# A graph-attention layer on one core: sums and edge values moved behind the queries, folds by halves, 53 pick blocks in six groups

## The chip, the cores and the metric

The kernel runs on one core of a Trainium2 chip. The time is that of the device from start to end, in microseconds (us); before, the median of three runs is 1701.03 us (1699.82 to 1702.28). Engines: TensorE (PE, with its weight loads as PEld), VectorE (DVE), ScalarE (ACT), GpSimd (POOL) and SyncE (SP), which here only issues transfers.

## The reference, cut to what matters

There are 6250 nodes with 64 features and 206,250 edges, sorted by destination. Each edge scores its source's key against its destination's query, weighted by its own attributes, in four heads of 16; the source's value times that score is summed per destination, and a layer norm follows.

```python
Qh = (x @ Wq.T + bq).reshape(n, H, D)        # H = 4, D = 16
Kh = (x @ Wk.T + bk).reshape(n, H, D)
Vh = (x @ Wv.T + bv).reshape(n, H, D)
Ee = (edge_attr @ We.T + be).reshape(-1, H, D)
score = (Kh[src] * Qh[dst] * (1.0 / np.sqrt(D)) * Ee).sum(-1)
score = jnp.exp(jnp.clip(score, -5.0, 5.0))
msg = Vh[src] * score[..., None]
wV = jax.ops.segment_sum(msg, dst, num_segments=n)
x = _layernorm(x + wV.reshape(n, H * D))
```

## The kernel before

**Tiles, groups, steps.** Edges are cut into 1612 tiles of 128 edges; 8 tiles make a group, 202 groups in all (the last has 4 tiles). Two groups make a step up to group 193; the last eight groups are steps of their own. One loop runs over the groups g (0 to 202), written out by hand as one order of instructions for every engine; each engine works through its own instructions in that order and waits on semaphores for the others.

**Keys and values of the sources.** A table with key and value of every node (`kv_tab`) is written at the start. For most tiles POOL fetches the 128 rows of a tile by one indirect DMA (`gather_kv`, line 276), four steps ahead, into a ring of five buffers (`kvs`). The first 40 tiles are computed from gathered rows of x. For the last two tiles of some groups (`PICKED`) there is no gather: PE makes the rows itself, as a product of the node features, kept in SBUF as three bf16 parts (`parts`), with one-hot columns. Four tiles form a batch of 512 edges; the 6250 nodes are 25 blocks per batch, and each block takes three matmuls of 512 columns (two for the last block), 74 in all: `picks`, which are the line 725 rows `pick<-hot,parts`. The one-hots are made by VectorE (`hots`, line 681) from the batch's source numbers, which SP fetches spread over the partitions (`fetch_sources`, tile `srcs`) and which ScalarE and VectorE turn into three forms (`sources`, lines 241 to 243). When a batch's 25 blocks are done, VectorE keeps the right half (`picked`, line 703), four f32 products with the weights give key and value (`picked_kv`, rows `pick<-w,x`), and ScalarE writes them into the group's buffer (`place_kv`).

How many blocks a group does is set by `first_unit`: 35 blocks in four groups, 8.75 per group. `READY` has the group in which a batch's last block is done; its four tiles are the last two of the groups `READY + 4` and `READY + 5`. `LAST`, the number of batches, is 67, which is 268 tiles, and 1304 tiles are left to the gathers. The last pick runs in group 192.

**The work of one group.** PE computes the edge values for group g + 3 (`edges`, four 64 x 64 quadrants of the array, rows `room<-et,we_sb`), the queries for g + 2 by one-hot rows (`queries`, rows `qq<-to,qw`, two halves of 64 columns), and the transposed terms for g + 1 (`turn`, line 761). ScalarE copies the edge values out with their bias (`biased`, line 740). VectorE multiplies them with the queries (`terms`, line 755), multiplies with the keys and sums per head (`products`, lines 787 and 789); ScalarE makes the weights (`weigh`, lines 794 and 796), VectorE the messages (`message`, line 808), which are split into three bf16 parts (`keep` on ScalarE, `take` on VectorE).

**Sums and folds.** For a step that is done, PE sums the messages per destination with one-hot matrices (`sums`, rows `room<-msg,of`, the two groups in the two column halves of the array in turn). VectorE adds the result into a ring of eight 64-row slots (`add`, lines 873 to 881). Every eight groups or so (25 times in the run) four slots are brought to the layout of the output by f32 matmuls (`fold_blocks`: for each half u one product with `fold` and one with a shifted part of `ident`), and VectorE adds them to y (`add_blocks`, line 927). Edge values, sums and folded blocks lie in the two PSUM banks of one tile, `room`.

**Order in one group, as far as the change touches it.** VectorE: products, take, terms, one-hots for the next group, messages, more one-hots, then the adds. PE: the first four blocks of picks, turn, queries, the other blocks of picks, fold, sums, edges. SP: edge attributes (every second group), source numbers, query windows, key rows. Gathers are released by marks on PE's matmuls (`where`), two to six of them per group.

Of the kernel before, what the change touches and what calls it, by code (L numbers as in the profile page):

```python
# [24 lines left out]
NG = -(-T // G)  # L25
# [47 lines left out]
UNITS = NB // 2  # L73
# [3 lines left out]
LEAD = 1  # L77
# [2 lines left out]

def first_unit(g):

    return (g - LEAD) * 35 // 4


def when(k):

    return max(g for g in range(LEAD + 4 * k // 35 + 2) if first_unit(g) <= k)


LAST = max(m for m in range(1, NG) if when(UNITS * m - 1) + 8 < NG)
BEGIN = [when(UNITS * m) for m in range(LAST)]
READY = [when(UNITS * m + UNITS - 1) for m in range(LAST)]
PICKED = [(READY[m] + 4, READY[m] + 5) for m in range(LAST)]
ALL_PICKED = {g for pair in PICKED for g in pair}
assert len(ALL_PICKED) == 2 * LAST and min(ALL_PICKED) > XG
assert all(BEGIN[m + 1] > BEGIN[m] + 1 for m in range(LAST - 1))
# [37 lines left out]
def tile_gnn(ctx: ExitStack, tc: tile.TileContext, x, x_blocks, by_rows, xT, wT, bias, beT, weT, eT, src, src_rows, dst,  # L135
# [96 lines left out]
    def fetch_sources(m, pool):  # L232

        if m < LAST:
            SRC[m] = pool.tile([P, BATCH * P], I32, name="srcs")
            nc.sync.dma_start(SRC[m], src_rows[m:m + 1, :].to_broadcast([P, BATCH * P]))
# [67 lines left out]
    with tc.tile_pool(name="nodes", bufs=1) as nodes, \  # L304
# [13 lines left out]
        slots = [kv.rearrange("p t c -> p (t c)") for kv in kvs]  # L318
# [13 lines left out]
        for i in range(NB // CB):  # L332
            s = slice(i * CB * P, (i + 1) * CB * P)
# [25 lines left out]
        mark = []  # L359
# [267 lines left out]
    with tc.If(rv == 0) as branch:  # L627

        with tc.tile_pool(name="work", bufs=2) as work, \
# [92 lines left out]
            mark = []  # L722
# [28 lines left out]
            def terms(g):  # L751

                n = tiles_of(g) // 2
                TERM[g] = work.tile([P, G // 2, P], F32, name="term")
                nc.vector.tensor_mul(TERM[g][:, :n], EB.pop(g)[:, :n], qq[:, :n])  # L755
# [24 lines left out]
            def some_of(g):  # L780

                n = tiles_of(g)
                return [(0, n)] if g < NG - 1 else [(0, n // 2), (n // 2, n)]
# [8 lines left out]
            def weigh(g, lo, hi):  # L792
                score = SCORE.pop(g)
                nc.scalar.activation(score, score, AF.Relu, bias=five_p, scale=-1.0)  # L794
                WEIGHT[g] = weights[g % 3][:, lo:hi]
                nc.scalar.activation(WEIGHT[g], score, AF.Exp, bias=five_p, scale=-1.0)  # L796
# [105 lines left out]
            def slots(lo, apart):  # L902

                ks = [k for k in (lo, lo + 2) if k in touched]
                if not apart and len(ks) == 2 and ks[0] % RING < ks[1] % RING:
                    return [(0, 2, ring[:, ks[0] % RING:ks[1] % RING + 1:2, :])]
                return [((k - lo) // 2, (k - lo) // 2 + 1, ring[:, k % RING:k % RING + 1, :]) for k in ks]

            def fold_blocks(i):

                for u in range(2):
                    whole = slots(4 * i + u, False)
                    for lo, hi, what in whole:
                        product(folded[u * C:(u + 1) * C, lo:hi], fold, what, start=True, stop=False,
                                skip_group_check=True)
                    for lo, hi, what in slots(4 * i + u - 1, i == len(ENDS) - 1):
                        product(folded[u * C:u * C + SHIFT, lo:hi], ident[:, C:C + SHIFT], what,
                                start=hi > max(h for _, h, _ in whole), stop=True, skip_group_check=True)

            def add_blocks(i):  # L920

# [61 lines left out]
            for g in range(NG + 1):  # L983
                now, before = g < NG, g > 0
                todo, ahead = pieces(g), pieces(g + 1)
                going, where = [], []
                if g < 2:
                    going = alone(lots(4)[2 * g:2 * g + 2])
                elif now and step_of[g] + KVB - 1 < NS:
                    going = lots(step_of[g] + KVB - 1)  # L990
                    going = alone(going[:2] if g == groups_of(step_of[g])[0] else going[2:])
                if g % LG == 0 and g + 3 * LG < NG:
                    fetch_edges(g // LG + 3)
                if g + 1 in BEGIN[1:]:
                    fetch_sources(BEGIN.index(g + 1) + 1, work)
                if g + 4 < NG:
                    fetch_queries(g + 4)
                if g % 2 == 0 and g + 6 < NG:
                    fetch_keys(g + 6, work)
                done = [s for s in range(NS) if groups_of(s)[-1] + 2 == g]  # L1000
                parted = now and step_of[g] < WHOLE
                former = before and step_of[g - 1] < WHOLE
                fetch_blocks(g)
                where.append(mark[-1])
                if former:
                    keep(g - 1, 1)
                if now:
                    products(g, *some_of(g)[0])
                if former:
                    take(g - 1, 1)  # L1010
                if g + 1 < NG:
                    terms(g + 1)
                if now:
                    weigh(g, *some_of(g)[0])
                if g + 2 < NG:
                    biased(g + 2)
                for mc in ahead[:1]:
                    hots(*mc)
                if now:
                    message(g, *some_of(g)[0])  # L1020
                for lo, hi in some_of(g)[1:] if now else []:
                    products(g, lo, hi)
                    weigh(g, lo, hi)
                    message(g, lo, hi)
                if g + 4 < NG:
                    onehot_rows(g + 4, work.tile([3 * W, G, P], BF16, name="to", bufs=4))
                if parted:
                    keep(g, 0)
                for mc in ahead[1:]:
                    hots(*mc)  # L1030
                for s in done:
                    add(s)
                if g - 1 in FOLDS:
                    add_blocks(FOLDS[g - 1])
                if g - 1 in READY:
                    picked(READY.index(g - 1))
                if g - 2 in READY:
                    picked_kv(READY.index(g - 2))
                    place_kv(READY.index(g - 2))
                where.append(mark[-1])  # L1040
                two = by_two(todo)
                for some in two[:2]:
                    picks(some)
                    where.append(mark[-1])
                if g + 1 < NG:
                    turn(g + 1)
                if g + 2 < NG:
                    queries(g + 2)
                for some in two[2:]:
                    picks(some)  # L1050
                    where.append(mark[-1])
                if g in FOLDS:
                    fold_blocks(FOLDS[g])
                if g - 1 in ends and now:
                    sums(ends[g - 1])
                if g + 3 < NG:
                    edges(g + 3)
                where.append(mark[-1])
                if g + 4 < NG:
                    onehot_rows_rest(g + 4)  # L1060
                if g in BEGIN:
                    sources(BEGIN.index(g) + 1, *from_odd())
                for i, lot in enumerate(going):
                    gather((lot, where[i * len(where) // len(going)]))
                for h in ([g] if g < NG - 3 else []) + ([g + 1] if NG - 4 <= g < NG - 1 else []):
                    if h not in ends:
                        continue
                    s = ends[h]
                    t0 = STEPS[s][0] * G
                    for t in range(t0, t0 + tiles_in(s)):  # L1070
                        if t and t % KEYS == 0:
                            keys(t)
                    onehot_edges(s)
                    if s >= WHOLE:
                        widen(s)
                if g - 1 in READY:
                    biased_kv(READY.index(g - 1))
                if parted:
                    take(g, 0)
                if done:  # L1080

                    while closed < B - 2 and summed[closed] <= g:
                        spreads(closed)
                        closed += 1
                    if closed in BATCHES and closed > scaled:
                        roots(scaled, closed)
                        scales(scaled, closed)
                        scaled = closed
                    for _ in range(3):
                        if normed < scaled:  # L1090
                            norm(normed)
                            normed += 1
# [180 lines left out]
```

## Time and profile before

| | before |
|---|---|
| median of three runs | 1701.03 us |
| the profiled execution | 1701.22 us |
| its span, first to last instruction | 1699.4 us |
| mean granted TensorE clock | 0.982 |
| busy: PE, VectorE, ScalarE, POOL | 1641.8, 1525.8, 1097.8, 1272.5 us |
| gathers (line 276) | 1304, mean 946 ns |
| pick matmuls | 4958 |

A line of the timeline has start, length, engine, line, operation, what is written and read with shapes, the number of merged instructions, and in brackets how long the engine was idle before and what ended that. A line of the waits has who waited for whom, the total in us, how many times, and the longest. A line of the groups has busy time and mean length, then the idle time before. Matmul ends are modelled, so starts are to be compared.

### The profile page before, as it was taken

Reading aid. Unit: us, or ns where it says so; the run is one execution under the profiler, and the core shown is the slowest. Engines: PE = TensorE matmul, PEld = TensorE weight load, DVE = VectorE, ACT = ScalarE, POOL = GpSimd, SP = SyncE. Lnnn points to the kernel's source line nnn. Section 1 sums busy time; section 2 is a strip of 40 time slices with the busy share of each in tenths; the row PEclk is TensorE's granted clock in tenths of the full one; section 3 lists DMA queues with packets and bytes.
Section 4 is the critical chain, followed back from the end, with each engine's and each line's share of the span. In section 5 each row is a group of like instructions: output and inputs, shape, how many; then the busy total and the mean of one; then the engine's idle time right before and its main releaser. Section 6 shows DMA issues by size and latency. Waiting matters only on the chain.

```text
span 1699.4 us, 29987 instructions
## 1 busy us (share of the span) xinstructions
PE 1641.8 (97%) x10327; PEld 818.4 (48%) x10327; DVE 1525.8 (90%) x2588; ACT 1097.8 (65%) x1860; POOL 1272.5 (75%) x1354
## 2 busy tenths in 40 slices
PE   7799999999999999999999999999999999999975
PEld 6444444444444444444444444444444444444443
DVE  5699989899989899998998998989999999889986
ACT  3676666666666666666666666666666666666664
POOL 7777777777777777777777777777777777777775
PEclk9799999999999999999999999999999999999995
DMA  6744344343443434434434344443444433434341
GB/s 195 244 123 143 99 123 123 104 124 109 114 123 104 123 108 114 124 117 123 114 108 130 99 122 122 106 124 105 117 123 117 123 111 111 123 105 130 111 116 46
DMA packets 115090, 203.90 MB, mean 120 GB/s; under 512 B 55216, under 2 KB 55961, under 8 KB 114815
## 3 DMA queue, kind: packets, MB, share of 16 engines
q1 hardware_dynamic: 71484, 113.99, 22.1%
q0 software_dynamic: 43008, 86.86, 19.3%
q8 instruction: 83, 1.36, 0.3%
q10 hardware_dynamic: 436, 1.04, 0.3%
q14 instruction: 79, 0.65, 0.1%
HBM read 194.18 MB, written 7.59 MB: 119 GB/s over the span
## 4 chain that ended last, share of the span: by engine, by line
PE 80%; DVE 7%; DMA 7%; issue 2%; ACT 2%; POOL 1%; SPq 0%; DVEq 0%; ACTq 0%; POOLq 0%
PE pick L725 59%; PE room L725 11%; PE qe L761 5%; DMA kv<-kv_tab,src_i 4%; PE qq L725 3%; DMA srcs<-in_src_rows 2%; POOL kv L276 1%; DVE prod L787 1%; DVE msg L827 1%; DVE term L755 1%; PE ps L490 1%; DVE hot L681 1%; DVE score L789 1%; DVE qe L827 1%; DVE of L775 1%
## 5 line engine op out<-in xcount | busy, mean ns | idle before, releaser
L276 POOL DMA_INDIRECT kv<-kv_tab,src_i x1304 | 1233.1, 946 | 398.1 <-issue 173.8
L725 PE MATMUL pick<-hot,parts 128*128 128x512 bf16 x4958 | 1136.4, 380 | 0.0
L725 PEld LDWEIGHTS <-parts 128*128 128x128 bf16 x4958 | 459.5, 98 | 588.1 <-issue 90.3
L681 DVE TENSOR_TENSOR hot<-from,still 128x2560 bf16<-128x2560 bf16 (+4 forms) x415 | 481.7, 1164 | 2.4 <-ACT still L796 2.4
L822 ACT ACTIVATE msg<-qe 128x512 bf16<-128x512 f32 x400 | 237.8, 594 | 170.2 <-DVE qe L808 98.8
L740 ACT ACTIVATE eb<-room,be_col 128x512 f32<-128x512 f32 x202 | 136.8, 677 | 147.1 <-PE room L725 146.6
L262 ACT ACTIVATE to<-to,one_p 126x1024 bf16<-126x1024 bf16 x198 | 226.9, 1146 | 0.0
L256 ACT ACTIVATE to<-kb,minus_row 126x1024 bf16<-126x1024 uint8 x198 | 224.7, 1135 | 0.0
L794 ACT ACTIVATE score<-score,five_p 128x32 f32<-128x32 f32 x203 | 65.1, 321 | 147.8 <-DVE score L789 145.9
L761 PE MATMUL qe<-ident,term 128*128 128x128 f32 x806 | 125.7, 279 | 28.1 <-DVE term L755 26.4
L787 DVE TENSOR_TENSOR prod<-kv,qe 128x512 f32<-128x512 f32 x203 | 137.1, 676 | 12.0 <-PE qe L761 3.7
L789 DVE TENSOR_REDUCE score<-prod 128x32 f32<-128x512 f32 x203 | 138.5, 682 | 7.0
L827 DVE TENSOR_TENSOR qe<-qe,msg 128x512 f32<-128x512 f32 x200 | 138.2, 691 | 3.9 <-ACT msg L822 3.8
L808 DVE SCALAR_TENSOR_TENSOR qe<-still,kv 128x512 f32<-128x512 f32 x200 | 138.7, 693 | 0.8 <-ACT still L796 0.8
L827 DVE TENSOR_TENSOR msg<-qe,msg 128x512 bf16<-128x512 f32 x200 | 136.6, 683 | 3.1 <-ACT msg L822 2.6
L755 DVE TENSOR_TENSOR term<-eb,qq 128x512 f32<-128x512 f32 x202 | 136.6, 676 | 3.0 <-DMA kv<-kv_tab,src_i 2.6
L725 PE MATMUL room<-et,we_sb 64*64 64x256 f32 (+1 forms) x1616 | 136.2, 408 | 0.3 <-ACT eb L740 0.2
L761 PEld LDWEIGHTS qe<-ident,term 128*128 128x128 f32 x806 | 99.9, 143 | 75.8 <-DVE term L755 41.9
L243 DVE TENSOR_SCALAR odd<-srcs 128x512 int32<-128x512 int32 x66 | 30.2, 458 | 79.4 <-DMA srcs<-in_src_rows 79.3
L725 PE MATMUL room<-msg,of 128*64 128x192 bf16 (+1 forms) x1592 | 88.6, 251 | 1.6 <-DVE y L927 1.3
L725 PEld LDWEIGHTS <-of 128*64 128x64 bf16 (+1 forms) x1600 | 67.4, 110 | 39.0 <-issue 36.6
L241 ACT ACTIVATE from<-srcs,from_row 128x512 bf16<-128x512 int32 x66 | 47.3, 717 | 60.0 <-DMA srcs<-in_src_rows 60.0
(156 smaller groups left out, 1102.9 us busy)
## 6 DMA issues: line engine op xcount, KB each, us to landing
et<-in_eT SPq DMA_DIRECT2D x100, 512.0 KB
kb<-key_tab SPq DMA_DIRECT2D x101, 252.0 KB
kv<-kv_tab,src_i POOLq DMA_INDIRECT x1304
srcs<-in_src_rows SPq DMA_DIRECT2D x67, 256.0 KB
qw<-q_tab SPq DMA_DIRECT2D x202, 15.8 KB
kv_tab<-kv_sb SPq DMA_DIRECT2D x4, 640.0 KB
q_tab<-q SPq DMA_DIRECT2D x5, 480.0 KB
out<-y SPq DMA_DIRECT2D x2, 512.0 KB
```

Of the source, the lines that this page charges most:

```text
L256: nc.scalar.activation(TO[g][:, :n, :], KB.pop(g)[:, :n * P].rearrange("p (j e) -> p j e", j=n), AF.Square, bias=minus_row3[:3 * W])
L262: nc.scalar.activation(TO[g][:, :n, :], TO[g][:, :n, :], AF.Relu, bias=one_p[:3 * W], scale=-1.0)
L276: return nc.gpsimd.indirect_dma_start(out=kv_of(g)[:, j, :], out_offset=None, in_=kv_tab[:, :], in_offset=bass.IndirectOffsetOnAxis(ap=src ...
L681: nc.vector.tensor_tensor(HOT[k][:, lo_ - lo:hi_ - lo].rearrange("p b (a c) -> p b a c", c=2), pairs(from_)[:, None].to_broadcast(shape), ...
L725: mark.append(nc.tensor.matmul(*aps, **kw))
L755: nc.vector.tensor_mul(TERM[g][:, :n], EB.pop(g)[:, :n], qq[:, :n])
L761: nc.tensor.transpose(qe[g % 2][:, k:k + half + 1:half, :], TERM[g][:, k, :], ident)
L787: nc.vector.tensor_mul(prod, kv_of(g)[:, lo:hi, :C], qe[g % 2][:, lo:hi, :])
L789: nc.vector.tensor_reduce(SCORE[g], prod.rearrange("p g (h d) -> p g h d", h=H), axis=AX.X, op=OP.add)
L808: nc.vector.scalar_tensor_tensor(to.rearrange("p g (h d) -> p g h d", h=H), WEIGHT.pop(g)[:, :, :, None].to_broadcast([P, n, H, D]), LEAST ...
L822: nc.scalar.activation(part, left, AF.Copy)
L827: nc.vector.tensor_sub(left if i == 0 else part_of(g, 2)[1], left, part)
```

## The change

- `first_unit`: 53 blocks in six groups (8.833 per group) in place of 35 in four. The bound on the last batch is looser (`+ 5` for `+ 8`), and the last batch's tiles may be nearer to its last block (`min(4, NG - 2 - r - 1)`), so that its groups are 199 and 200. There are 69 batches; the last pick runs in group 196.
- `fold_blocks`: both halves' products with `fold` first, then both shifted ones.
- `fetch_sources`: issued two groups ahead of its use, not one.
- VectorE: the adds (`add`, `add_blocks`) stand right after the terms, ahead of one-hots and messages, and in the written order ahead of ScalarE's copy of the edge values.
- In group 200 the products stand behind the terms of group 201, not ahead of them.
- PE: fold, sums and edges come right behind the queries, ahead of the group's remaining picks.

```diff
 def first_unit(g):
-    return (g - LEAD) * 35 // 4
+    return (g - LEAD) * 53 // 6
 def when(k):
-    return max(g for g in range(LEAD + 4 * k // 35 + 2) if first_unit(g) <= k)
+    return max(g for g in range(LEAD + 6 * k // 53 + 2) if first_unit(g) <= k)
-LAST = max(m for m in range(1, NG) if when(UNITS * m - 1) + 8 < NG)
+LAST = max(m for m in range(1, NG) if when(UNITS * m - 1) + 5 < NG)
-PICKED = [(READY[m] + 4, READY[m] + 5) for m in range(LAST)]
+PICKED = [(r + k, r + k + 1) for r in READY for k in [min(4, NG - 2 - r - 1)]]
...
             def fold_blocks(i):
+                whole = [slots(4 * i + u, False) for u in range(2)]
                 for u in range(2):
-                    whole = slots(4 * i + u, False)
-                    for lo, hi, what in whole:
+                    for lo, hi, what in whole[u]:
                         product(folded[u * C:(u + 1) * C, lo:hi], fold, what, start=True, stop=False,
                                 skip_group_check=True)
+                for u in range(2):
                     for lo, hi, what in slots(4 * i + u - 1, i == len(ENDS) - 1):
                         product(folded[u * C:u * C + SHIFT, lo:hi], ident[:, C:C + SHIFT], what,
...
-                if g + 1 in BEGIN[1:]:
-                    fetch_sources(BEGIN.index(g + 1) + 1, work)
+                if g + 2 in BEGIN[1:]:
+                    fetch_sources(BEGIN.index(g + 2) + 1, work)
...
-                if now:
+                if now and g != NG - 2:
                     products(g, *some_of(g)[0])
                 if former:
                     take(g - 1, 1)
                 if g + 1 < NG:
                     terms(g + 1)
+                if g == NG - 2:
+                    products(g, *some_of(g)[0])
                 if now:
                     weigh(g, *some_of(g)[0])
+                for s in done:
+                    add(s)
+                if g - 1 in FOLDS:
+                    add_blocks(FOLDS[g - 1])
                 if g + 2 < NG:
                     biased(g + 2)
...
                 for mc in ahead[1:]:
                     hots(*mc)
-                for s in done:
-                    add(s)
-                if g - 1 in FOLDS:
-                    add_blocks(FOLDS[g - 1])
...
                 if g + 2 < NG:
                     queries(g + 2)
-                for some in two[2:]:
-                    picks(some)
-                    where.append(mark[-1])
                 if g in FOLDS:
                     fold_blocks(FOLDS[g])
                 if g - 1 in ends and now:
                     sums(ends[g - 1])
                 if g + 3 < NG:
                     edges(g + 3)
+                for some in two[2:]:
+                    picks(some)
+                    where.append(mark[-1])
                 where.append(mark[-1])
```

More of the change, by code (lines that the diff above doesn't have):

```diff
@@ L909, in fold_blocks @@
             def fold_blocks(i):
+                whole = [slots(4 * i + u, False) for u in range(2)]
                 for u in range(2):
-                    whole = slots(4 * i + u, False)
-                    for lo, hi, what in whole:
+                    for lo, hi, what in whole[u]:
                         product(folded[u * C:(u + 1) * C, lo:hi], fold, what, start=True, stop=False,
                                 skip_group_check=True)
+                for u in range(2):
                     for lo, hi, what in slots(4 * i + u - 1, i == len(ENDS) - 1):
                         product(folded[u * C:u * C + SHIFT, lo:hi], ident[:, C:C + SHIFT], what,
-                                start=hi > max(h for _, h, _ in whole), stop=True, skip_group_check=True)
+                                start=hi > max(h for _, h, _ in whole[u]), stop=True,
+                                skip_group_check=True)
             def add_blocks(i):
```

## The prediction

> **What bounds the kernel now.** I read the page first, then the waits, the queue of gathers in order of time, and the end of the run engine by engine. The page alone points at PE:
>
> ```profile
> span 1699.4 us, 29987 instructions
> PE 1641.8 (97%) x10327; PEld 818.4 (48%) x10327; DVE 1525.8 (90%) x2588; ACT 1097.8 (65%) x1860; POOL 1272.5 (75%) x1354
> L276 POOL DMA_INDIRECT kv<-kv_tab,src_i x1304 | 1233.1, 946 | 398.1 <-issue 173.8 <-PE pick L725 83.2 <-DMA kv<-kv_tab,src_i 66.7
> ```
>
> POOL's 75% misleads. 398.1 us of idle time over 1304 gathers is 0.305 us each, and the waits of POOL have nothing longer than that; rows of its timeline 28 gathers apart give the step:
>
> ```profile
> POOL kv L276 <- PE pick L725: 83.2, 273, 0.3
> ...
> 1650.14 0.94 POOL L276 DMA_INDIRECT kv<-kv_tab,src_i  x1 [0.30 <-issue]
> ...
> 1685.08 0.95 POOL L276 DMA_INDIRECT kv<-kv_tab,src_i  x1 [0.30 <-issue]
> ```
>
> (1685.08 - 1650.14) / 28 = 1.248 us per gather, 0.94 of it busy and 0.30 between two. So POOL issues gathers without a break, 1304 x 1.248 = 1627 us of them, up to 1686.0. Nothing in the run holds it back, and only fewer gathers shorten it. Whether that stream ends the run is seen in VectorE's timeline of the tail:
>
> ```profile
> 1636.64 0.69 DVE L787 TENSOR_TENSOR prod<-kv,qe 128x512 f32<-128x512 f32 x1
> ...
> 1683.09 0.69 DVE L787 TENSOR_TENSOR prod<-kv,qe 128x512 f32<-128x512 f32 x1 [3.13 <-issue]
> ...
> 1685.34 0.69 DVE L808 SCALAR_TENSOR_TENSOR kv<-still,kv 128x512 f32<-128x512 f32 x1
> ...
> 1693.88 0.32 DVE L955 TENSOR_SCALAR y<-y,stats,rstd 128x64 f32<-128x64 f32 x1
> ```
>
> The product at 1683.09 is that of group 200. The last gather for it is the fifth from the end (1685.08 - 4 x 1.248 = 1680.1, done at 1681.0, landed some 2 us later): VectorE sat 3.13 us for it. From there to the end of the span are 16.3 us. So before ends on the gathers, but with 3.1 us of slack only: PE, whose picks stop in group 192, is close behind. Both have to be priced.
>
> PE's tail, the turns of iterations 192 and 196, and the last sums but one:
>
> ```profile
> 1636.00 0.60 PE L761 MATMUL qe<-ident,term 128*128 128x128 f32 x4
> ...
> 1656.63 1.11 PE L761 MATMUL qe<-ident,term 128*128 128x128 f32 x4 [3.17 <-DVE term L755]
> ...
> 1687.24 3.57 PE L725 MATMUL pick<-kv,kv 128*128 128x64 f32 x16
> ```
>
> PE's timeline in the middle of the run, iterations back to back:
>
> ```profile
> 835.13 1.16 PE L725 MATMUL pick<-w,x 128*128 128x128 f32 x8
> 836.13 2.75 PE L725 MATMUL pick<-hot,parts 128*128 128x512 bf16 x12
> ...
> 842.93 0.43 PE L725 MATMUL room<-ring,fold 128*64 128x128 f32 x2
> 843.29 0.41 PE L725 MATMUL room<-ring,ident 128*31 128x64 f32 x4
> 843.63 0.43 PE L725 MATMUL room<-ring,fold 128*64 128x128 f32 x2
> 844.00 0.41 PE L725 MATMUL room<-ring,ident 128*31 128x128 f32 x2
> 844.33 0.85 PE L725 MATMUL room<-msg,of 128*64 128x192 bf16 x16
> 845.11 0.66 PE L725 MATMUL room<-et,we_sb 64*64 64x256 f32 x8
> 845.71 2.55 PE L725 MATMUL pick<-hot,parts 128*128 128x512 bf16 x11
> 848.09 0.60 PE L761 MATMUL qe<-ident,term 128*128 128x128 f32 x4
> 848.62 0.41 PE L725 MATMUL qq<-to,qw 126*64 126x512 bf16 x2
> 848.96 3.41 PE L725 MATMUL pick<-hot,parts 128*128 128x512 bf16 x15
> 852.30 0.66 PE L725 MATMUL room<-et,we_sb 64*64 64x256 f32 x8
> 852.89 2.76 PE L725 MATMUL pick<-hot,parts 128*128 128x512 bf16 x12
> ```
>
> Starts are what counts, as the ends are modelled. 11 picks followed by the turn take 848.09 - 845.71 = 2.38, so 0.2164 each. 15 picks followed by the edges take 852.30 - 848.96 = 3.34 against 15 x 0.2164 = 3.25: leaving the picks for narrow tiles costs 0.094. The two query matmuls (512 columns, one column half each) take 0.34 before the picks, where one stream of 512 columns is 0.216: going back to the picks costs 0.124.
>
> **The change, part by part.**
>
> *53 blocks in six groups.* 8.833 blocks per group in place of 8.75; with the looser bound on the last batch 69 batches of 25 blocks in place of 67. A batch is 24 x 3 + 2 = 74 picks and spares 4 gathers. POOL: 1304 - 8 = 1296 gathers, 8 x 1.248 = 10.0 us less. PE: 148 picks x 0.2164 = 32.0 us, two more blocks of eight f32 matmuls (836.13 - 835.13 = 1.0) 2.0 us. The picks now end in group 196, so four more iterations stand ahead of that point: each turn, queries and edges, 0.53 + 0.34 + 0.59 = 1.46, is 5.8, three sums at 0.78 and one fold at 1.40 are 3.7. Together the turn of iteration 196 would come at 1636.0 + 43.5 = 1679.5, were nothing saved.
>
> *Sums and edge values behind the queries.* In an iteration the picks were left for the sums or edges (0.094) and entered from the queries (0.124); now both go, and the step from queries to sums or to edges is new. The trace has no such step. Bounds: 0 (sums use the same column halves as the queries) and 0.124 (the dearest switch seen). To the edges I take 0.094, as from the picks, to the sums 0; sums come in every second iteration. Saved: 0.124 or 0.218, mean 0.171, in 195 iterations 33.3 us; ends 18.3 and 42.5. The Trainium skill ("TensorEngine Tiling (Array Packing)", Key Properties) says that a change of tiling mode drains the array and a change of tile does not; the 0.094 on leaving the picks agrees with it, and by it the sums' step is free and the edges' is not: 33.3 us again, with the low end out.
>
> *Folds by halves in turn.* A fold is 844.33 - 842.93 = 1.40 us: 0.36, 0.34, 0.37, 0.33. Halves do run side by side here: 16 sums of 192 columns take 0.78, one after the other they would be 16 x 192/512 x 0.2164 = 1.30. At best half of 1.40 goes, at worst nothing; each f32 product shows as two records, of which I expect one to overlap, so 0.35 in 24 folds, 8.4 us (0 to 16.8). The Trainium skill ("TensorE: Matmul & The Clock Gate", Part 3, The mechanism) has matmuls start and end strictly in program order; if the two records of a half stay next to each other, that too gives about half; no run here shows it yet.
>
> PE's sum: 1679.5 - 33.3 - 8.4 = 1637.8 for the turn of iteration 196 (ends 1620 and 1661). From that turn before took 1699.4 - 1656.63 = 42.8 us, of which 3.13 were the gather: 39.7. PE alone would end at 1677.5.
>
> *POOL's sum.* Product of group 200 at 1683.09 - 10.0 = 1673.1, and 16.3 after it: 1689.4. It is later than PE's 1677.5, so it decides, as long as PE's savings are over 30 us of the 41.7 I expect. What is late next is then the gathers again, and PE waits for them from about group 190 on.
>
> *Terms of the last group ahead of products (g = 200).* Its turn and the sums before then no longer stand behind the gather; the sums at 1687.24 could start with the messages at 1685.34 + 0.69 = 1686.03. 0 to 1.2 us; I take 1.0. Span 1688.4.
>
> *Source rows a group further ahead; adds right after the weights.* Rows of the waits, the fourth of the window 1560 to 1700 alone, the last of SP's queue:
>
> ```profile
> DVE odd L243 <- DMA srcs<-in_src_rows: 79.3, 35, 3.7
> ACT from L241 <- DMA srcs<-in_src_rows: 60.0, 37, 2.9
> PE qe L761 <- DVE term L755: 26.4, 19, 5.4
> ...
> PE qe L761 <- DVE term L755: 20.6, 8, 5.4
> ...
> SPq L216 <- PE room L725: 1177.7, 87, 18.7
> ```
>
> SP issues in bursts: the edge load waits for a PE edge block, and source rows, queries and keys go behind it. A fetch one group earlier leaves with the burst before where it was late, and with the same burst, early enough, where it was not. So VectorE's 79.3 us go; they were paid by slack mostly, PE waited 26.4 us in all for VectorE, 20 of it in the tail. I count nothing. The added work of VectorE and ScalarE is hidden by that:
>
> ```profile
> 800.00:1000.00 200.00, 199.28 (x1278) 96.45 (x1277) 182.57 (x294) 129.85 (x216) 151.23 (x161) 1.00 0.41 118
> ```
>
> (Columns: window, PE, PE's weight loads, VectorE, ScalarE, POOL.) And the timeline of one iteration:
>
> ```profile
> 846.28 0.38 SPq L236 DMA_DIRECT2D srcs<-in_src_rows  x1
> ...
> 850.34 0.43 DVE L243 TENSOR_SCALAR odd<-srcs 128x512 int32<-128x512 int32 x1 [2.71 <-DMA srcs<-in_src_rows]
> ...
> 855.04 0.68 DVE L755 TENSOR_TENSOR term<-eb,qq 128x512 f32<-128x512 f32 x1
> 855.14 0.67 ACT L740 ACTIVATE eb<-room,be_col 128x512 f32<-128x512 f32 x1
> ...
> 855.63 1.48 DVE L681 TENSOR_TENSOR hot<-from,still 128x2560 bf16<-128x2560 bf16 x1
> ...
> 855.77 0.66 PE L761 MATMUL qe<-ident,term 128*128 128x128 f32 x4
> ```
>
> 50 more blocks of one-hots at 1.48 / 5 = 0.30 are 15 us of VectorE in 1640, against 79 freed; without that cover VectorE, busy 182.57 of 200, would still be under POOL's pace. Two more fetches on SP (256 KB each) and ACT's two batches are idle time. The adds move ahead of one-hots and messages, which come under 1 us later, with the next picks over 4 us away.
>
> **The whole.** Span 1688.4 against 1699.4; outside the span lie 1701.22 - 1699.4 = 1.8 us, so 1690.2, and the profiled run was 0.2 over the median of 1701.03: 1690.0 us, 0.65% faster. About 0.2% (3.4 us) is what a measurement can tell from no change.
>
> **Rivals.**
>
> 1. *PE decides.* If the new step from queries costs the dearest switch everywhere and the folds win nothing, 18.3 us are saved, the turn is at 1661.2 and the end at 1661.2 + 39.7 - 1.0 = 1699.9, a time of 1701.7: no change. From 18 to 30 us saved the time falls from there to 1690. For it: PE's 97%. Against it: both switches are there in the rows above.
>
> 2. *A new wait in PE's queue; slower.* Sums and edges write the two banks that ScalarE's copy of the edge values (line 740) reads, and 15 picks now queue behind them. In the rows above that copy ends at 855.81 and the turn came at 855.77, sums or edges would want the banks 0.53 + 0.34 = 0.87 us after that: it suffices by 0.8. But the add, which reads the same banks, is now put ahead of the copy; if the copy waits for it, it comes about 0.4 later, after folds 1 us. Slower than before from 1677.5 - 1.0 + w over 1699.4 + 3.4, w = 26 us, 0.13 per iteration. At 0.35 in every second iteration, 34 us, the time is 1712. Against it: PE waited for VectorE's term only 19 times in 202, so it mostly runs behind, with the copy long done.
>
> 3. *The fetch is not earlier* (the burst still holds it), so VectorE keeps its 79.3 us: 182.57 + 9.3 of 200 us busy or waiting is 0.96 of the pace, still under POOL's. Time 1690 as well; it changes nothing here.
>
> **How the numbers follow.** POOL decides: 0.70 (rival 3 within it), 1688.5 to 1692. PE decides: 0.15, spread over 1691 to 1702. New wait: 0.12, 1702 to 1715. Anything else, 0.03. The range 1687 to 1700 leaves out rival 2 and the end of rival 1. Faster by 0.2%: 0.70 and over half of 0.15, 0.78; within 0.2%: 0.08; slower: 0.14.
>
> **What would show it.** Gathers x1296, still without a wait over 0.3, their last near 1676; picks x5106; the queries followed by sums within about 0.22 and by edges within about 0.31; a fold under 1.1; the waits for srcs nearly gone; a product of groups 195 to 200 that waits for a gather. Wrong: PE's row of waits with an entry for eb (line 740) or the add over 20 us, POOL rows with gaps over 0.3 in the middle, or picks that run to 1665 and no wait for gathers after them.

## The result, and the profile after

The changed kernel takes 1691.5 us, the median of six runs (1690.68 to 1692.92), against 1701.23 us (1699.82 to 1702.69, six runs) before: a ratio of 0.9943, 95% interval 0.993 to 0.9956. The profiled execution took 1691.6 us.

The page of the kernel after, its head and its costliest rows:

```profile
span 1689.7 us, 30289 instructions
PE 1623.6 (96%) x10491; PEld 842.8 (50%) x10491; DVE 1533.3 (91%) x2593; ACT 1106.1 (65%) x1870; POOL 1265.5 (75%) x1346
L276 POOL DMA_INDIRECT kv<-kv_tab,src_i x1296 | 1226.1, 946 | 395.2 <-issue 196.8
L725 PE MATMUL pick<-hot,parts 128*128 128x512 bf16 x5106 | 1148.8, 380 | 0.0
```

There are 1296 gathers and 5106 picks. 395.2 us of idle time over 1296 gathers is 0.305 us each, the same short gap as before: POOL still issues without a break. Its last gather, in its timeline after, and its longest row of waits for PE (total, times, longest):

```profile
1675.06 0.94 POOL L276 DMA_INDIRECT kv<-kv_tab,src_i  x1 [0.30 <-PE pick L725]
...
POOL kv L276 <- PE pick L725: 82.6, 271, 0.3
```

It ends at 1676.0, against 1686.0 before: the 10.0 us that eight gathers are worth. The stream starts at the same time in both (its first gather at 55.1 before and at 55.0 after). VectorE's timeline of the tail after, the products of the groups 196 to 200:

```profile
1642.93 0.69 DVE L787 TENSOR_TENSOR prod<-kv,qe 128x512 f32<-128x512 f32 x1 [1.54 <-PE pick L725]
...
1650.79 0.69 DVE L787 TENSOR_TENSOR prod<-kv,qe 128x512 f32<-128x512 f32 x1 [2.00 <-DMA kv<-kv_tab,src_i]
...
1659.94 0.68 DVE L787 TENSOR_TENSOR prod<-kv,qe 128x512 f32<-128x512 f32 x1
...
1666.96 0.68 DVE L787 TENSOR_TENSOR prod<-kv,qe 128x512 f32<-128x512 f32 x1
...
1674.07 0.68 DVE L787 TENSOR_TENSOR prod<-kv,qe 128x512 f32<-128x512 f32 x1
```

The product of group 200 starts at 1674.07, and 15.6 us later the span ends. The last product that waited for its gather is not this one but that of group 197, at 1650.79. From there the products come 9.15, 7.02 and 7.11 us apart. In a later run, in which the gathers do not decide (after with fewer gathers and the folds of before), the same products start at 1629.76, 1639.13, 1646.15 and 1653.27, so 9.37, 7.02 and 7.12 us apart: the last three groups run at their own pace, started by a gather. The gather for group 200, the fifth from the end, started at 1670.07. Before, the product followed the start of that gather by 3.0 us (1683.09 - 1680.09), so here the gather would have let it start at 1673.1, 1.0 us before it did. How long the products waited in all is in VectorE's waits after, first of the window 110 to 780, then of 780 to 1690:

```profile
DVE prod L787 <- PE qe L761: 22.2, 28, 1.8
```

```profile
DVE prod L787 <- PE pick L725: 32.9, 22, 4.6
DVE prod L787 <- DMA kv<-kv_tab,src_i: 30.2, 14, 5.0
DVE prod L787 <- PE qe L761: 3.9, 4, 1.5
```

Up to 780 us products waited for PE alone; behind it they waited for the gathers. The row that names the picks belongs with them, as a later run shows. The pace says the same. Two windows with the products (L787) alone, of the kernel before and then of the kernel after, give their number in brackets:

```profile
200.00:700.00 500.00, 42.09 (x62) 1.00 0.40 114
900.00:1600.00 700.00, 58.89 (x87) 1.00 0.41 116
```

```profile
200.00:700.00 500.00, 43.60 (x64) 1.00 0.42 118
900.00:1600.00 700.00, 57.86 (x85) 1.00 0.41 115
```

After, a group takes 500 / 64 = 7.8 us early and 700 / 85 = 8.2 later; before it took 500 / 62 = 8.06 and 700 / 87 = 8.05. A group after needs 8 - 4 x 8.833 / 25 = 6.587 gathers on average, and 6.587 x 1.248 = 8.22 us, which is the later pace. So PE now runs ahead at its own pace, uses up the stock of gathered rows, and is then held to the pace of the gathers. The stream of gathers decides the end, as before, but PE would now be done long before it, where it was close behind it.

### The profile page after: what moved, and what is told of

Same layout as the page of the kernel before. It is cut to its first block, busy times and chain, and to the rows that moved or that the text cites. A ratio compares the mean times of both kernels' runs of the same rounds, so it can differ in the third digit from the quotient of the medians.

```text
span 1689.7 us, 30289 instructions
## 1 busy us (share of the span) xinstructions
PE 1623.6 (96%) x10491; PEld 842.8 (50%) x10491; DVE 1533.3 (91%) x2593; ACT 1106.1 (65%) x1870; POOL 1265.5 (75%) x1346
## 4 chain that ended last, share of the span: by engine, by line
PE 80%; DVE 10%; issue 4%; DMA 3%; ACT 2%; POOL 0%; DVEq 0%; SPq 0%; ACTq 0%; POOLq 0%
PE pick L725 60%; PE room L725 10%; PE qe L761 5%; PE qq L725 3%; DMA kv<-kv_tab,src_i 2%; DVE hot L681 2%; DVE prod L787 1%; DVE msg L827 1%; DVE term L755 1%; PE ps L490 1%; DVE qe L808 1%; DVE score L789 1%; DVE qe L827 1%; DMA ones_tab<-ones 0%; DMA et<-in_eT 0%
## 5 line engine op out<-in xcount | busy, mean ns | idle before, releaser
L276 POOL DMA_INDIRECT kv<-kv_tab,src_i x1296 | 1226.1, 946 | 395.2 <-issue 196.8
L725 PE MATMUL pick<-hot,parts 128*128 128x512 bf16 x5106 | 1148.8, 380 | 0.0
L725 PEld LDWEIGHTS <-parts 128*128 128x128 bf16 x5106 | 484.0, 98 | 618.0 <-issue 77.9
L681 DVE TENSOR_TENSOR hot<-from,still 128x2560 bf16<-128x2560 bf16 (+4 forms) x414 | 492.9, 1195 | 2.5 <-ACT still L796 2.4
L787 DVE TENSOR_TENSOR prod<-kv,qe 128x512 f32<-128x512 f32 x203 | 137.4, 677 | 96.1 <-PE pick L725 32.9
L725 PE MATMUL qq<-to,qw 126*64 126x512 bf16 x396 | 80.9, 405 | 0.0
L725 PEld LDWEIGHTS <-of 128*64 128x64 bf16 (+1 forms) x1600 | 73.8, 110 | 14.1 <-issue 5.0
L725 PEld LDWEIGHTS pick<-w,x 128*128 128x128 f32 x552 | 72.1, 192 | 15.6 <-ACT pick L714 6.7
```

The lines of the kernel that those rows point to most:

```text
L276: return nc.gpsimd.indirect_dma_start(out=kv_of(g)[:, j, :], out_offset=None, in_=kv_tab[:, :], in_offset=bass.IndirectOffsetOnAxis(ap=src ...
L681: nc.vector.tensor_tensor(HOT[k][:, lo_ - lo:hi_ - lo].rearrange("p b (a c) -> p b a c", c=2), pairs(from_)[:, None].to_broadcast(shape), ...
L725: mark.append(nc.tensor.matmul(*aps, **kw))
L787: nc.vector.tensor_mul(prod, kv_of(g)[:, lo:hi, :C], qe[g % 2][:, lo:hi, :])
```

## The experiments

The first eight of the runs fell on two chips on which before itself takes 2047 us, with PE's matmuls spread out by pauses that no wait explains; each run is compared with before on its own chip. The last four were on a chip where before takes 1705.83 us (1703.33 to 1709.6, 14 runs).

**The order without the new blocks.** The new order, folds and fetches, with the pick schedule of before (67 batches, 1304 gathers):

```diff
-    return (g - LEAD) * 53 // 6
+    return (g - LEAD) * 35 // 4
...
-LAST = max(m for m in range(1, NG) if when(UNITS * m - 1) + 5 < NG)
+LAST = max(m for m in range(1, NG) if when(UNITS * m - 1) + 8 < NG)
```

> All of the new order, but 35 blocks in four groups as before: 67 batches, 1304 gathers. Theory A (the gathers end the run, PE's savings are slack): POOL's stream is 10.0 us longer than after's again, so about 1691.5 + 10 = 1701, at best 1 us less for the reordered last group; 1700 to 1701.5, no gain that can be measured. Theory B (PE ends the run and its shorter order is the gain): after's PE work less 148 picks, 32 us, about 1660.

> The order-only kernel (35 blocks in four groups, 67 batches, 1304 gathers) once more, for a chip on which before takes about 1700 us; the chip of the first four runs took 2047 for it, with pauses in PE's own stream, and there order only was 1.0004 of before. Theory A (the gathers end the run): 1304 gathers end at 1686 as before, 1700 to 1701.5. Theory B (PE ends it): about 1660. If pauses stand in PE's stream again, neither: within 0.2% of before.

Measured: 2048.71 us, ratio 1.0004 (0.9993 to 1.0016), and on the second chip 2048.46, 1.0002 (0.9984 to 1.0021). No change, as expected where gathers decide; but these chips can't say that it is for this reason. PE's timeline of the second run:

```profile
783.55 0.35 PE L725 MATMUL room<-msg,of 128*64 128x192 bf16 x3
784.23 0.29 PE L725 MATMUL room<-msg,of 128*64 128x192 bf16 x2 [0.33 <-issue]
784.95 0.24 PE L725 MATMUL room<-msg,of 128*64 128x192 bf16 x1 [0.43 <-issue]
...
790.50 1.13 PE L725 MATMUL room<-et,we_sb 64*64 64x256 f32 x8
```

The 16 sums took 790.50 - 783.55 = 6.95 us; before, in the prediction's rows, they took 0.78. In the rows shown the first of them start some 0.7 us apart, and the engine waited for nothing that the profile shows. POOL is not full here either; from the page of the same run:

```profile
L276 POOL DMA_INDIRECT kv<-kv_tab,src_i x1304 | 1238.6, 950 | 719.0 <-issue 307.4
```

719.0 / 1304 = 0.55 us idle before each gather, against 0.305 in the prediction's row.

**The new blocks without the order.** The kernel before with the new `first_unit`, `LAST` and `PICKED` alone:

```diff
-    return (g - LEAD) * 35 // 4
+    return (g - LEAD) * 53 // 6
...
-PICKED = [(READY[m] + 4, READY[m] + 5) for m in range(LAST)]
+PICKED = [(r + k, r + k + 1) for r in READY for k in [min(4, NG - 2 - r - 1)]]
```

> The order of before with 53 blocks in six groups: 69 batches, 1296 gathers, no other part of the change. Theory A alone (fewer gathers are the gain): 1691. My sum has PE decide here, as nothing pays for the 43.5 us of added work: the turn of iteration 196 at 1679.5, then 39.7 us and 1.8 outside the span, 1721, slower by 1.2%. Theory B: the same 1721.

> The picks-only kernel (order of before, 69 batches, 1296 gathers) once more, for a chip on which before takes about 1700 us. Gathers alone: 1691. My sum: PE decides, turn of iteration 196 at 1679.5, then 39.7 and 1.8: 1721. On a chip with pauses: 1.004 of before as in the first run.

Measured: 2055.54 us, 1.004 (1.0027 to 1.0052), and 2056.44, 1.0035 (1.0013 to 1.0058). Eight gathers less, and slower. The prediction's working has the turn at 1679.5 without any saving, 1679.5 + 39.7 = 1719.2 for the span, 1.2% over before; the direction is that, the size is a third, on chips where pauses stretch PE's work.

**The picks back between queries and sums**, the rest as after:

```diff
+                for some in two[2:]:
+                    picks(some)
+                    where.append(mark[-1])
                 if g in FOLDS:
                     fold_blocks(FOLDS[g])
...
-                for some in two[2:]:
-                    picks(some)
-                    where.append(mark[-1])
```

> After, with the rest of the picks back between the queries and the fold, sums and edges; folds, adds, source rows and 69 batches stay. By my sum PE loses the switches it had saved (0.15 to 0.17 per iteration, 29 to 33 us) and only the folds pay (0.73 x 24 = 17.5): turn of iteration 196 at 1679.5 - 17.5 = 1662, then 38.7, span 1700.7, time 1698 to 1702.5. If the gathers still decide: 1691.5. Theory B (all of it on PE's path): 1691.5 + 30 = 1721.

Measured: 2048.56 us, 1.0013 (0.9998 to 1.0028). Not told apart from before on that chip.

**More blocks still**, 55 in six groups, 71 batches, in the new order:

```diff
-    return (g - LEAD) * 53 // 6
+    return (g - LEAD) * 55 // 6
```

> After, with 55 blocks in six groups: 71 batches, 1288 gathers, picks to group 194. Theory A: POOL's stream is 8 x 1.248 = 10 us shorter, PE has 148 picks and two batches' f32 products more, 34 us, against about 41 us that it now loses waiting for gathers (7.81 us per group up to group 89, 8.2 after): both end close together, 1682 to 1686, faster than after. Theory B or VectorE near its limit: 1691.5 + 10 to 34, slower than after.

> After with 55 blocks in six groups (71 batches, 1288 gathers) once more, for a chip on which before takes about 1700 us. Theory A: gathers and PE end close together, 1682 to 1686. If PE or VectorE is the limit at that point: 1692 to 1725. On the chip with pauses it was 0.994 of before.

Measured: 2035.28 us, 0.994 (0.9916 to 0.9963), and 2034.91, 0.9939 (0.9913 to 0.9965). Faster than before there; the kernel after was not run on those chips and this one not on a quiet chip, so whether it beats after stays open.

**After with fewer gathers.** In the groups 20 to 193 one gather per group is left out (174 in all, so the values of these tiles are stale):

```diff
-            js = [j for j in range(tiles_of(g)) if not is_picked(g, j)]
+            js = [j for j in range(tiles_of(g)) if not is_picked(g, j) and (j or not 20 <= g < 194)]
```

> After, but in groups 20 to 193 the first tile's keys and values are not gathered: 174 gathers left out, so those tiles use what the buffer holds from an earlier group and the output is not the reference's. POOL then has 217 us less to do and cannot end the run. Theory A: PE and VectorE now set the pace; at the 7.81 us per group that after has up to group 89, the turn of iteration 196 comes 40 us sooner and the run ends at about 1650 (1645 to 1660; my sum in the prediction gave 1679). Theory B (gathers never mattered): 1691.5.

Measured, on the second of the two chips: 1824.39 us, 0.8906 (0.8865 to 0.8947), which is 223 us less than before there. Divided by the 174 gathers that is 1.28 us each, but the run differs from before by the whole change as well, and after itself was not run there. Against the order alone on the same chip (2048.46 us, 182 gathers more) it is 1.23 us each. PE's waits ahead of picks for nothing visible come to 58.3 us here and to 100.4 in the run of the order alone, so on these chips the pauses of PE shrink when gathers go. What links the two was not found, and the sizes of these eight runs are therefore not carried over to the chip of the result. The next four runs are on a chip without the pauses.

**After itself, there.**

> The changed kernel itself on the chips of these experiments, where before takes 2047 us. The pace of the five kernels seen here goes with the gathers per group (6.6: 9.82 us, 6.53: 9.73, 5.59: 8.50, whatever PE's order), not with PE's work. If that holds for after (6.587 gathers per group, order of after): 9.80 us per group, its tail shorter than that of order only, 2036 to 2042, ratio 0.994 to 0.998. If PE's work decides: 32 us more picks than order only, 2080. Order only and picks only add up to 1.004.

Measured: 1691.4 us (1690.75 to 1692.17), 0.9915 (0.9898 to 0.9931). POOL's timeline of this run:

```profile
1675.38 0.94 POOL L276 DMA_INDIRECT kv<-kv_tab,src_i  x1 [0.30 <-issue]
```

The expectation was meant for the chips with pauses, and this chip has none, so the run does not test it. The last gather ends at 1676.3, on the chip of the result at 1676.0. Before differs by 4.6 us between the two chips (1701.23 and 1705.83), after by 0.1, as it should be if its end hangs on a stream of gathers of fixed length. The expectations of the next three runs, too, are in the times of the chips with pauses; only their differences can be compared, and after with fewer gathers alone was not run here.

**Before with fewer gathers**, the same 174 left out as above:

> Before, with the same 174 gathers left out as in the run of after with fewer gathers (those tiles use what the buffer holds, the output is not the reference's). With the gathers out of the way PE's path decides on both: after had 1824.4 here. By my sum before has 41.7 us of switches and folds more (with a fold gain of 0.73, as the trace of after has it, 47) and 34 us of picks less, also VectorE's waits for source rows: 1832 to 1845. If PE's order is worth nothing when matmuls pause: 1790 (the picks alone).

Measured: 1702.75 us (1696.98 to 1706.69), 0.9984 (0.9969 to 0.9998). Its page and waits:

```profile
span 1700.3 us, 29468 instructions
L276 POOL DMA_INDIRECT kv<-kv_tab,src_i x1130 | 1068.7, 946 | 559.6 <-PE pick L725 212.1 <-issue 155.9 <-PE room L725 79.1
...
DVE odd L243 <- DMA srcs<-in_src_rows: 86.7, 35, 4.0
PE qe L761 <- DVE term L755: 25.6, 22, 4.0
```

POOL now sits for PE's marks, 212.1 us of it and up to 2.7 us at a time, where before had 0.3 at most. So the gathers don't end this run, PE does, and it is only 3.1 us shorter (interval 0.3 to 5.3). Before had its two bounds within a few us of each other. Fewer gathers alone would have bought next to nothing.

**After with fewer gathers and the folds of before**: what PE does when it alone decides.

```diff
-            js = [j for j in range(tiles_of(g)) if not is_picked(g, j)]
+            js = [j for j in range(tiles_of(g)) if not is_picked(g, j) and (j or not 20 <= g < 194)]
...
                 for u in range(2):
-                    for lo, hi, what in whole[u]:
+                    whole = slots(4 * i + u, False)
+                    for lo, hi, what in whole:
...
-                for u in range(2):
                     for lo, hi, what in slots(4 * i + u - 1, i == len(ENDS) - 1):
```

> After with fewer gathers (174 left out, as above) and the folds in the old order: u = 0 whole and shifted, then u = 1. Prediction's term: 0.35 x 24 = 8.4 us; by the starts in the trace of after (fold to sums 0.67 in place of 1.40) 17.5 us: 1824.4 + 8.4 = 1833 or + 17.5 = 1842. If PE is not what decides here: 1824.

Measured: 1670.68 us (1670.05 to 1670.73), 0.9793 (0.9777 to 0.981). From its page, waits and timeline of PE:

```profile
span 1668.9 us, 29791 instructions
...
DVE prod L787 <- PE qe L761: 60.5, 72, 2.1
...
PE qe L761 <- DVE term L755: 9.0, 4, 4.0
...
1629.12 0.60 PE L761 MATMUL qe<-ident,term 128*128 128x128 f32 x4
```

20.7 us less than after on this chip, although the slow folds are back: PE doesn't end the kernel after, the gathers do. Products now wait for PE (60.5 us), and PE waits for VectorE's terms 9.0 us, nearly all of it in the last groups. The 32.9 us that after's waits put down to picks are gone from the run with the gathers; so they were waits for gathers. PE at its own pace has the turn of iteration 196 at 1629.1. A fold in this run, and then one in the kernel after, from PE's timelines:

```profile
884.35 0.38 PE L725 MATMUL room<-ring,fold 128*64 128x128 f32 x2
884.66 0.40 PE L725 MATMUL room<-ring,ident 128*31 128x128 f32 x2
885.00 0.43 PE L725 MATMUL room<-ring,fold 128*64 128x128 f32 x2
885.36 0.40 PE L725 MATMUL room<-ring,ident 128*31 128x128 f32 x2
885.69 0.85 PE L725 MATMUL room<-msg,of 128*64 128x192 bf16 x16
```

```profile
1630.10 0.39 PE L725 MATMUL room<-ring,fold 128*64 128x128 f32 x4
1630.42 0.42 PE L725 MATMUL room<-ring,ident 128*31 128x64 f32 x6
1630.77 0.85 PE L725 MATMUL room<-msg,of 128*64 128x192 bf16 x16
```

885.69 - 884.35 = 1.34 us one half after the other, 1630.77 - 1630.10 = 0.67 in turn: the second half adds no time. The other folds of the two traces agree (1.34 to 1.36, but for a smaller one at the end, and 0.65 to 0.67). In 24 folds that is 16 us.

**After with fewer gathers and the picks back between**, the new folds kept:

```diff
-            js = [j for j in range(tiles_of(g)) if not is_picked(g, j)]
+            js = [j for j in range(tiles_of(g)) if not is_picked(g, j) and (j or not 20 <= g < 194)]
...
+                for some in two[2:]:
+                    picks(some)
+                    where.append(mark[-1])
                 if g in FOLDS:
...
-                for some in two[2:]:
-                    picks(some)
-                    where.append(mark[-1])
```

> After with fewer gathers (174 left out, as above) and the rest of the picks back between the queries and the fold, sums and edges. Prediction's term: 0.171 x 195 = 33.3 us (18.3 to 42.5); by the steps in the trace of after, queries to sums 0.237 and to edges 0.333, it is 0.15 per iteration, 29 us: 1824.4 + 29 = 1853 (1843 to 1867). If PE is not what decides here: 1824.

Measured: 1699.36 us (1699.31 to 1699.53), 0.996 (0.9942 to 0.9977). From its page and waits:

```profile
span 1697.7 us, 29804 instructions
...
ACT eb L740 <- DVE still L873: 125.3, 74, 3.1
DVE still L873 <- PE room L725: 93.1, 72, 2.5
...
PE qe L761 <- DVE term L755: 13.3, 8, 4.0
```

1697.7 - 1668.9 = 28.8 us more than the run before it here, which has the new order but not the new folds. With 16 us for the folds, the order of PE is worth some 45 us, if the two add up, where 29 were expected. It is the largest part of the change by far, and most of it can't be seen in the time: this run, with PE deciding, takes 1699.36 us, and after, where the gathers decide, 1691.4 on the same chip, so of the 45 us at least 8 show, and the rest is hidden behind the gathers. For the same reason before with fewer gathers lies further behind than expected: 8 to 21 us over after with fewer gathers were expected, and 1700.3 - (1668.9 - 16) is 47 (an estimate, as the second term was not run).

## Why the prediction was right, and where it was not

The time (1690.0 said, 1691.5 measured) and the reason (the gathers decide) hold. There is luck in it: the prediction left 1689.4 - 1677.5 = 12 us between the gathers' end and PE's, and its sum for PE was off by about twice that. The error was on the harmless side; as large the other way, PE would have decided. That the eight gathers are the gain is read from the timelines and from the run that takes gathers away; the new order with the old 1304 gathers was not run on a chip without pauses. Point by point:

- *POOL's sum.* 1296 gathers at the same step, 10.0 us sooner as worked out. The longest of their waits is not 0.3, as read off one row, but 0.5 (another row, of waits for nothing visible), before and after alike; it doesn't change the sum. The product of group 200 came at 1674.07, 1.0 later than said, and it did not wait for its gather: the wait came three groups earlier, and the tail's own pace led from there. The number is close because the two limits lie 1.0 us apart.
- *Before ends on the gathers with PE close behind.* The run of before with fewer gathers, 0.2% faster, agrees. On that chip PE's end comes some 4 us later (1700.3 of span, where the prediction's rows give 1699.4 - 3.1 = 1696.3 without the wait), so it confirms that the bounds are close, not the 3.13 us to the decimal.
- *Switches on PE, 33.3 us.* PE's timeline after:

```profile
836.78 0.60 PE L761 MATMUL qe<-ident,term 128*128 128x128 f32 x4
837.31 0.41 PE L725 MATMUL qq<-to,qw 126*64 126x512 bf16 x2
837.65 0.66 PE L725 MATMUL room<-et,we_sb 64*64 64x256 f32 x8
838.24 5.35 PE L725 MATMUL pick<-hot,parts 128*128 128x512 bf16 x24
843.43 0.60 PE L761 MATMUL qe<-ident,term 128*128 128x128 f32 x4
843.96 0.41 PE L725 MATMUL qq<-to,qw 126*64 126x512 bf16 x2
844.20 0.83 PE L725 MATMUL room<-msg,of 128*64 128x192 bf16 x16
844.96 0.66 PE L725 MATMUL room<-et,we_sb 64*64 64x256 f32 x8
845.56 3.41 PE L725 MATMUL pick<-hot,parts 128*128 128x512 bf16 x15
848.80 1.05 PE L725 MATMUL pick<-w,x 128*128 128x128 f32 x8
849.70 2.75 PE L725 MATMUL pick<-hot,parts 128*128 128x512 bf16 x12
```

  Queries to sums take 844.20 - 843.96 = 0.24, which is 0.024 over the lone 0.216; queries to edges 837.65 - 837.31 = 0.34, 0.12 over. I had taken 0 and 0.094. Saved are 0.218 - 0.024 = 0.19 or 0.218 - 0.12 = 0.10, mean 0.15, 29 us in 195 iterations: within the prediction's bounds, 4 us under its value. The rule of the Trainium skill ("TensorEngine Tiling (Array Packing)", Key Properties), that a change of tiling mode drains the array and a change of tile does not, agrees: 0.024 without a change of mode, 0.12 with one. The run with the old folds has two more cases: a fold (128x64, like the queries) starts 0.24 behind the queries, and the sums of the last groups, which use the whole array (128x128), start 0.34 behind them.
- *Folds, 8.4 us: mis-sized, measured 16 to 17.5.* Half of the time goes from every fold, 0.73 of 1.40 against before. I expected one of the two records of each f32 product to overlap, from the rule that matmuls start and end strictly in program order (the Trainium skill, "TensorE: Matmul & The Clock Gate", Part 3, The mechanism) and the thought that the two records of a half stay next to each other. The trace shows full overlap of the halves; how the records are interleaved it doesn't show.
- *PE's sum, 1637.8 for the turn of iteration 196: too late.* Without the folds' gain it was 1646.2, and the run with fewer gathers and the old folds had it at 1629.1, 17.1 us sooner. PE alone would end after's span near 1668.9 - 16 = 1653 (worked out from that run, not measured), where 1676.5 was said, the 1.0 us of the tail taken off. Of these 24 us the folds are 8 and the order of PE 12 (45 against 33.3); the other 4 lie in the rest of the sum, and if PE ends some 4 us later on that chip in this run too, they are rather 8. The early source rows, priced at nothing, may be among them (two points on). Within the order's 45 the switches make 29. The f32 products of a batch now lie inside a stream of picks and take 849.70 - 848.80 = 0.90 in place of 1.00, 7 us in 69 batches. With the picks between, the early adds wait for sums that are queued late (93.1 us in that run's waits), and the copy of the edge values waits for the adds; little of it reached PE, which waited for terms 13.3 us there against 9.0 with the new order. The last 5 are not assigned.
- *"PE waits for the gathers from about group 190 on": wrong.* The gathers bind from about 780 us, near group 91. The prediction's own figures would already have put it earlier: 8.06 us per group before, plus 34.0 for picks and less 41.7 saved over 195 groups, is 8.02 for PE against 8.22 for the gathers, so the 12 us between the two ends build up over some 60 groups, from about group 140 on (an estimate). The rest is that PE was faster than its sum, 7.8 us per group early. This changed nothing of the time: PE's saving beyond what the gathers allow is hidden.
- *Source rows a group ahead, counted at nothing.* The waits of VectorE and ScalarE for `srcs`, 79.3 and 60.0 us before, have no entry after, which settles rival 3: the fetch is earlier. How much they held PE back was not tried alone. Between 110 and 1590 us PE waited for VectorE's terms 8.9 us in the run of before with fewer gathers (VectorE waits 86.7 us for source rows there), and not at all in the run with the old folds. By these waits it may have been up to some 9 us, not nothing.
- *The tail, 1.0 us for the terms ahead of the products.* From the product of group 200 to the end were 16.3 us and are 15.6: 0.7.
- *Rival 1, PE decides:* fell with the run that has fewer gathers and the old folds: PE still had its work, and the time fell by 20.7 us. *Rival 2, a new wait in PE's queue:* the wait is there, but PE hardly feels it. From the waits after:

```profile
ACT eb L740 <- DVE still L873: 61.2, 73, 1.1
...
PE qe L761 <- DVE term L755: 33.0, 26, 4.6
...
PE room L725 <- ACT eb L740: 2.0, 5, 0.8
```

  The copy of the edge values waits for the early add in 73 iterations, up to 1.1 us, as that rival had it; PE's sums and edges waited for the copy 2.0 us in all, where the rival needed 26.

## What to carry to other kernels

An engine that is 75% busy can be the bound: divide its idle time by its instructions, and if the gap is the same short one each time, only fewer instructions help, and only as far as the next bound allows. When two engines end a run within a few us of each other, relieve both in one change, and price each against the other's end: here fewer gathers alone brought 0.2%, and of PE's savings, some 60 us where the gathers are out of the way (45 and 16, if they add up), most stays hidden behind the gathers. On PE, put matmuls of the same narrow tiling next to each other, and let the two column halves take turns.

## What the runs showed of the hardware that was not expected

- The f32 products of the two column halves of the array, issued in turn, take 0.67 us together, as long as those of one half alone (half of 1.34).
- Behind the queries (128x64) the next matmuls start after 0.24 us where they are tiled alike (sums, folds), and after 0.34 where they are not (edge values on 64x64, sums on 128x128); one stream of 512 columns takes 0.216.
- On two chips the same program takes 2047 us in place of 1701. In stretches PE's small matmuls start 0.7 us apart there, without a wait in the profile, and with gathers left out the run is shorter by more than 1.2 us for each, although POOL idled 0.55 us before each, more than on the chip of the result. The granted clock is 0.94 to 0.95 for before there, against 0.98; those 4% alone can't make 20% of the time. What the pauses are stays open.
